# A graph layer's gathered rows: five or four tiles a batch by columns instead of four or three, more column groups on VectorE, and the weighting in three pieces

## The chip, the cores and the metric

The kernel runs on one core of a Trainium2 chip. The metric is the time of one execution on the device, in microseconds (us); a time of a kernel is the median of its runs. The profile is one execution of its own.

## The reference

The layer has 12,500 nodes with 128 features and 412,500 edges, sorted by target (`dst`). Cut to what matters:

```python
x = x + layer(relu(layernorm(x)), [src, dst], edge_attr)

def layer(node_features, edge_indices, edge_features, W_node, W_edge, a):   # 4 heads of 32
    h = (node_features @ W_node.T).reshape(num_nodes, H, HD)
    e = (edge_features @ W_edge.T).reshape(num_edges, H, HD)
    h_src, h_tgt = h[src], h[tgt]
    att = jnp.sum(jnp.concatenate([h_src, h_tgt, e], axis=-1) * a, axis=-1)
    att = jnp.where(att > 0, att, 0.2 * att)
    m = jnp.maximum(segment_max(att, tgt), 0.0)
    ex = jnp.exp(att - m[tgt])
    denom = segment_sum(ex, tgt) + (num_edges - deg)[:, None] * jnp.exp(-m)
    w = ex / denom[tgt]
    return segment_sum(w[:, :, None] * h_src, tgt)
```

So each edge needs one row of `h` (its source's), a score, the largest score of its target, and a weighted sum into its target.

## The kernel before

**Tiles and batches.** A first stage makes a table of rows (144 floats: four heads and their scores) for all nodes. Then the edges go by in 461 chunks of 896; seven chunks make a batch, 66 batches in all. A batch holds 49 tiles of 128 rows × 144, in one of three buffers `hs`. Four ways fill a tile of `hs` with the rows of its sources:

- POOL's indirect DMA, `gather_tile` (L334), one instruction a tile: 44 tiles in an odd batch, 45 in an even one.
- SP, row by row (`row_by_row`, DMAs at L864): one tile a batch, 128 rows in an odd batch and 96 in an even one, in groups of 32 rows. One group goes ahead of each load of edge features `eft` (`load`, L760), on the same queue.
- By columns: the normalised node features lie transposed in on-chip memory (`features`), so that one node is one column. `column_by_column` takes a group of 32 source numbers into registers (a load at L852) and copies 32 columns, one by one, into `turned`: by DVE (L883) or by ACT (L885). `put_back` then multiplies a tile of `turned` with the weights on PE (L904) into `more`, of which there is one, and ACT copies it into `hs` (L905). `TURNED = 4`: an odd batch has four such tiles (16 groups), an even one three and a quarter (13 groups; the quarter, 32 rows of SP's tile, goes through L909 and L911).
- The tile by rows and the tiles by columns are left out of POOL's list (`apart_of`, `clear_rows`).

**A batch on the engines.** The program has one hand-written order for all engines. In iteration `b`: SP loads indices, near rows and penalties; POOL waits at a small memset (`gate`, L819) until the scatter of batch b − 2 is done, and gathers batch b + 1; SP goes through the rows of batch b + 2 and its `eft`. Then `weigh(b)` on DVE: logits (L1000, L1001), sums (L1004, four), the leaky step (L1007, L1008), a scan up (L1009), a scan down (L1012), the subtraction (L1014). ACT takes the exponential (L1016, four), and DVE goes on with L1018 (four), a transpose that waits for the exponential (L1021) and L1026.

Behind it come the put-backs of batch b + 2 (`later`), one by one: the first behind the exponential, the second behind ACT's loads of `near_dst`, then a group of columns, the third, and the fourth where there is one. Then `collect(b − 1)`: 16 copies on ACT (L1120) that take the sums of the batch before out of PE's accumulator, with a group of columns in the middle. Then `scatter(b)`: DVE multiplies the rows with the weights (L1089) in two pieces, tiles 0 to 2 and 2 to 7 of each chunk, and 28 matmuls of PE (L1095 in the profile) sum them by target; each waits for its piece and, the first, for `collect`. DVE makes addresses (L842) and masks (L789) for later batches. Behind every even batch's scatter two batches are merged (`close`; ACT L1167 and L1168, DVE L1151 to L1194). At the end of the iteration come ACT's remaining groups, and PE begins the scores of batch b + 2 (L935, L938), which wait for its `eft`.

**Who copies the groups.** `OF_SCALAR = (10, 9)`: ACT has 10 groups in an even iteration and 9 in an odd one: one ahead of the last put-backs, one inside `collect`, two ahead of an even iteration's merge or with the rest, and the rest at the end, ahead of the next exponential. `OF_VECTOR = (5, 5)`: DVE has one group behind each of the first five places of `BEHIND`: "rows" and "first" (behind the two pieces of the product), "near" (behind L789), "hot" (behind L958) and "down" (behind the second scan L1012, ahead of the subtraction L1014).

The exponential of a batch thus stands behind all of ACT's groups of the iteration before, and DVE's subtraction behind its group.

Of the kernel before, what the change touches and what calls it, by code (L numbers as in the profile page):

```python
# [25 lines left out]
T = 7  # L26
# [41 lines left out]
FIRST = 2  # L68
# [6 lines left out]
PLACE = 88736  # L75
HOME = 11104
ALL = NBT - 7
TURNED = 4
OF_SCALAR = (10, 9)
OF_VECTOR = (5, 5)  # L80
BEHIND = ("rows", "first", "near", "hot", "down", "up")


def tiles_of(c):
# [75 lines left out]
def kernel(  # L160
# [195 lines left out]
    with (  # L356
# [140 lines left out]
        def of_vector(u):  # L497
            return (u.s.b0 + u.i0) // XS % 3 == 0 and u.m == XS
# [425 lines left out]
    def on_half(s, step):  # L924

        tc.declare_no_dep(step.ins, group=f"z{s.b + 1}", reason="the next batch has other partitions")
        tc.add_manual_dep(step.ins, s.made.ins.name, mybir.DependencyInfo(mybir.DependencyClass.Sync, mybir.DependencyReason.DATA))
# [63 lines left out]
    def weigh_part(s, t0, t1):  # L991

        zst, att, up, m, both = s.zst, s.att, s.up, s.m, s.both
        own = s.hs.rearrange("p (t q) (h k) -> p t q h k", t=T, h=H)[:, t0:t1, :s.chunks, :, AW - 1]
        e0, e1 = t0 * P, t1 * P

        def grouped(what, g):
            return what.rearrange("r (t g i) -> r g t i", g=NQT, i=R)[:, g, t0:t1, :]

        nc.vector.tensor_copy(logits[:, t0:t1, :s.chunks * H].rearrange("p t (q h) -> p t q h", h=H), own)  # L1000
        nc.vector.transpose(zst[:, t0:t1, :].rearrange("p t i -> p (t i)"),  # L1001
                            logits[:, t0:t1, :].rearrange("p t i -> p (t i)"))
        for g in range(NQT):
            on_half(s, nc.vector.tensor_tensor(grouped(up, g), grouped(s.z, g),  # L1004
                                               zst[g * R:(g + 1) * R, t0:t1, :], op=OP.add))
        z = s.z[:, e0:e1]
        nc.vector.tensor_scalar(att[:, e0:e1], up[:, e0:e1], 0.2, None, op0=OP.mult)  # L1007
        on_half(s, nc.vector.tensor_tensor(z, up[:, e0:e1], att[:, e0:e1], op=OP.max))  # L1008
        on_half(s, nc.vector.tensor_tensor_scan(up[:, e0:e1], s.pen[:, e0:e1], z, 0.0, op0=OP.add, op1=OP.max))  # L1009
        of_vector("up")  # L1010
        mp = m[:, e0:e1]
        nc.vector.tensor_tensor_scan(mp[:, ::-1], s.pen[:, e1:e0:-1], up[:, e0:e1][:, ::-1], 0.0, op0=OP.add, op1=OP.max)  # L1012
        of_vector("down")
        on_half(s, nc.vector.tensor_tensor(att[:, e0:e1], z, mp, op=OP.subtract))  # L1014
        for g in range(NQT):
            nc.scalar.activation(both[g * R:(g + 1) * R, 0, t0:t1, :], grouped(att, g), AF.Exp)  # L1016
        for g in range(NQT):
            nc.vector.scalar_tensor_tensor(both[g * R:(g + 1) * R, 1, t0:t1, :], grouped(s.pen[:, 1:], g), -1.0 / BIG,  # L1018
                                           grouped(up, g), op0=OP.mult, op1=OP.mult)
        if t1 - t0 == T:  # L1020
            nc.vector.transpose(both_ps.rearrange("p w t r -> p (w t r)"), both.rearrange("p w t r -> p (w t r)"))  # L1021
        else:
            for w in range(2):
                nc.vector.transpose(both_ps[:, w, t0:t1, :].rearrange("p t r -> p (t r)"),  # L1024
                                    both[:, w, t0:t1, :].rearrange("p t r -> p (t r)"))
        nc.vector.tensor_copy(own, both_ps[:, 1, t0:t1, :s.chunks * H].rearrange("p t (q h) -> p t q h", h=H))  # L1026
# [56 lines left out]
    def scatter(s):  # L1083

        flat = s.hs.rearrange("p i c -> p (i c)")
        blocks = flat.rearrange("p (t x k) -> p t x k", t=T, k=HS)
        for t0, t1 in ((0, FIRST), (FIRST, T)):
            rows = blocks[:, t0:t1, :, :HB]
            nc.vector.tensor_tensor(  # L1089
                rows, rows, ex_ps[:, t0:t1, :CB * H, None].to_broadcast([P, t1 - t0, CB * H, HB]), op=OP.mult)  # L1090
            of_vector("rows" if t1 == T else "first")
            for t in range(t0, t1):
                for g in range(2):
                    at = (t * CB + g * NEXT) * ROW + g * HALFROW
                    scattered[s.b] = nc.tensor.matmul(  # L1095
                        wide_ps[:, g, :], s.hot[:, t, g * NEXT:g * NEXT + SB, :].rearrange("p q r -> p (q r)"),
                        flat[:, at:at + SPAN], start=(t == 0), stop=(t == T - 1))
                    if s.fence:
                        tc.declare_no_dep(scattered[s.b].ins, s.fence, reason="DVE's products are behind that wait")
# [171 lines left out]
    def batch(b):  # L1271
        if b not in batches:
            s = batches[b] = Batch()
            s.b = b
            s.hs = None
            s.turned, s.groups = None, []
            s.c0 = chunk_of(b)
            s.chunks = chunk_of(b + 1) - s.c0
        return batches[b]
# [27 lines left out]
    with tc.manual_schedule():  # L1307
# [20 lines left out]
        for b in range(NBT - 1):  # L1328
            s = batch(b)
            batches.pop(b - 3, None)  # L1330
            soon = b >= NBT - ALONE
            if AHEAD <= b + 3 < NBT:
                batch(b + 3).ends = index(b + 3)
            load_near(batch(b + 1))
            load_pen(batch(b + 1))
            due = [k for k in (b - 1,) if k >= 0 and k < NBT - ALONE and merge_of(k)[1] == k]
            for k in due:
                for b0, n, behind in parts():
                    if behind == k and not held_x:
                        held_x[b0] = load_part(work, b0, n)  # L1340
            if b:
                gather(batch(b + 1), scattered.get(b + 1 - RING))
            if b + 2 < NBT:
                open_rows(batch(b + 2))
            if b + 4 < NBT:
                number(batch(b + 4))
            if b + 2 < NBT:
                load(batch(b + 2), True)
            if b == NBT - 2:
                choose(batch(b + 1))  # L1350
                mark(batch(b + 1))
            spare[ENG.Activation] = OF_SCALAR[b % 2] if b <= BOTH else 0
            chosen.clear()
            chosen.update(BEHIND[:OF_VECTOR[b % 2] if b <= BOTH else 0])
            weigh(s)
            later = batch(b + 2) if b + 2 < NBT else None
            if later:
                put_back(later, 0)
            if b < NBT - 2:
                mark(s)  # L1360
            for store in stores:
                store()
            stores.clear()
            if later:
                load_dst(later, nc.scalar)
                put_back(later, 1)
            of_scalar()
            if later:
                put_back(later, 2)
                put_back(later, 3)  # L1370
            if 1 <= b <= NBT - ALONE:
                collect(batch(b - 1))
            if later:
                put_back(later, TURNED)
            scatter(s)
            if b + 4 < NBT:
                address(batch(b + 4))
            if b < NBT - ALONE:
                choose(batch(b + 1))
            if 1 <= b <= NBT - ALONE:  # L1380
                if merge_of(b - 1)[1] == b - 1:
                    of_scalar(2)
                close(batch(b - 1))
            if soon:
                collect(s)
                if b == NBT - 2:
                    first_part(batch(b + 1))
            if NBT - ALONE <= b < NBT - 2:
                choose(batch(b + 1))
            if b == NBT - 3:  # L1390
                mark(batch(b + 1))
            of_scalar(spare[ENG.Activation])
            assert all(k.b > b + 3 for k, _, _ in turning), b
            if b + 2 < NBT:
                begin(batch(b + 2))
            if b == COUNTED:
                add_windows(count_windows())
            if b == 1:
                nc.scalar.copy(acc.rearrange("p q d -> p (q d)"), carry_m.to_broadcast([P, WQ * AW]))
                near_columns()  # L1400
            if soon:
                for b0, n, behind in parts():
                    if behind == b and not held_x:
                        held_x[b0] = load_part(work, b0, n)
                close(s)
            if b + 2 < NBT:
                clear_rows(batch(b + 2))
# [294 lines left out]
```

## Time and profile before

| what | us |
|---|---|
| median of 3 runs | 6768.51 |
| lowest and highest | 6765.73 and 6787.56 |
| the profiled execution | 6719.83 |
| its span (first to last instruction) | 6718.1 |

The busy times are of the span. A row of the waits names the engine, the tile and line that waited, the engine, tile and line that released it, and then the total in us, how often, and the longest. "issue" as the releaser means that the engine waited for nothing that the profile shows. A row of a timeline has the start, the duration, the engine, line and operation, the tiles written and read, and how many instructions are drawn together; in brackets the engine's idle time ahead of it and its releaser. DVE, ACT, POOL, PE and SP are the five engines; SPq and ACTq are DMA starts on their queues. Line numbers of the changed kernel are those of before up to L1008 and one higher from L1009 on.

### The profile page before, as it was taken

The page shows a single profiled execution, that of the slowest core. Times are in us where ns is not written, and L with a number is a line of the kernel's source. Part 1 is how long each engine was busy: PE and PEld are TensorE (multiplying, and loading weights), DVE is VectorE, ACT ScalarE, POOL GpSimd, SP SyncE. Part 2 cuts the span into 40 slices and gives each one's busy share as a digit, 9 for nine tenths or more (in the row PEclk, how much of TensorE's full clock was granted, in tenths as well). Part 3 has the DMA queues.
Part 4 walks back from the last instruction along what each step waited for, and adds up shares of the span by engine and source line. Part 5 has one row for each costly group of instructions (what it writes and reads, how often), then busy time and mean ns, then how long its engine had stood idle before and what let it go on. Part 6 is the DMA issues. An engine that isn't in the chain of part 4 may idle for free. (4 is left out here: it accounts for less than half of the span.)

```text
span 6718.1 us, 65140 instructions
## 1 busy us (share of the span) xinstructions
PE 1803.4 (27%) x4569; PEld 724.3 (11%) x4569; DVE 2718.8 (40%) x13514; ACT 2583.9 (38%) x20492; POOL 2797.8 (42%) x3018
## 2 busy tenths in 40 slices
PE   4223123223123232222232232133123223312323
PEld 3101001011011011010011011011011001101111
DVE  4434334344344243353343344344334334434445
ACT  4134334334344344344344344344334434433420
POOL 4453443343443443533533443443453353344351
PEclk8566566566566566665666566566566566656666
DMA  4322222222222222222222222222222222222221
GB/s 115 94 61 58 61 61 64 61 61 62 57 63 65 59 64 60 64 65 57 64 66 61 65 66 61 62 63 61 67 64 65 59 61 67 62 66 65 64 66 43
DMA packets 225620, 432.22 MB, mean 64 GB/s; under 512 B 92316, under 2 KB 125094, under 8 KB 225144
## 3 DMA queue, kind: packets, MB, share of 16 engines
q0 software_dynamic: 94240, 216.84, 13.5%
q1 hardware_dynamic: 100664, 145.09, 7.4%
q10 hardware_dynamic: 30240, 66.08, 2.8%
q14 instruction: 438, 3.59, 0.2%
q8 instruction: 38, 0.62, 0.0%
HBM read 412.21 MB, written 15.53 MB: 64 GB/s over the span
## 5 line engine op out<-in xcount | busy, mean ns | idle before, releaser
L885 ACT COPY turned<-features 128x1 f32 x18624 | 2053.1, 187 | 3473.0 <-issue 3469.9
L334 POOL DMA_INDIRECT hs<-table,ends x2887 | 2734.6, 947 | 1006.8 <-issue 895.0
L819 POOL MEMSET gate<- 128x1 f32 x63 | 6.2, 99 | 2758.7 <-PE pa L1095 2751.6
L1095 PE MATMUL pa<-hs,hot 128*128 128x504 f32 x1820 | 937.0, 680 | 531.5 <-ACT r L1120 478.6
L904 PE MATMUL more<-wall,turned 128*128 128x144 f32 x430 | 155.5, 457 | 3011.5 <-ACT hs L905 2985.0
L883 DVE COPY turned<-features 128x1 f32 x9888 | 681.8, 142 | 691.9 <-issue 689.8
L1021 DVE STREAM_TRANSPOSE exr<-both 128x448 f32<-128x448 f32 x65 | 42.9, 660 | 1530.4 <-ACT both L1016 1529.8
L1095 PEld LDWEIGHTS pa<-hs,hot 128*128 128x128 f32 x1820 | 398.5, 223 | 1045.4 <-issue 505.2
L1089 DVE TENSOR_TENSOR hs<-hs,exr 128x1848 f32<-128x1848 f32 (+1 forms) x130 | 456.6, 3515 | 0.0
L904 PEld LDWEIGHTS more<-wall,turned 128*128 128x128 f32 x430 | 91.5, 265 | 3093.8 <-ACT hs L905 3027.1
L938 PE MATMUL z<-eft,wa 128*32 128x512 f32 (+1 forms) x792 | 354.4, 592 | 61.5 <-DMA eft<-in_ef 61.4
L935 PE MATMUL z<-eft,wa 128*64 128x512 f32 (+1 forms) x132 | 85.6, 738 | 960.1 <-DMA eft<-in_ef 814.5
L1014 DVE TENSOR_TENSOR a<-z,a 32x896 f32<-32x896 f32 (+1 forms) x67 | 71.7, 1070 | 643.5 <-issue 643.3
L1120 ACT COPY r<-pa 32x70 f32<-32x70 f32 (+1 forms) x1040 | 263.6, 253 | 119.3 <-PE pa L1095 88.2
L1004 DVE TENSOR_TENSOR up<-z,zst 32x224 f32<-32x224 f32 (+2 forms) x268 | 104.3, 389 | 429.8 <-PE z L795 418.9
L795 PE MATMUL z<-near_dst,near_rows 128*32 128x512 f32 (+1 forms) x528 | 214.7, 550 | 30.5 <-DVE run L1154 22.6
L1018 DVE SCALAR_TENSOR_TENSOR both<-pen_sb,up 32x224 f32<-32x224 f32 (+2 forms) x268 | 100.3, 374 | 202.2 <-issue 201.7
L1016 ACT ACTIVATE both<-a 32x224 f32<-32x224 f32 (+2 forms) x268 | 102.8, 384 | 172.1 <-DVE a L1014 126.1
L789 DVE TENSOR_TENSOR near_dst<-near_dst,least 128x1792 f32<-128x1792 int32 x66 | 132.4, 2006 | 20.3 <-DMA near_dst<-in_dstc 20.3
L958 DVE TENSOR_TENSOR hot<-exr,key 128x1568 f32<-128x1568 f32 x65 | 116.4, 1791 | 59.3 <-PE pa L1095 57.1
L1009 DVE TENSOR_TENSOR_SCAN up<-pen_sb,z 32x896 f32<-32x896 f32 (+1 forms) x67 | 133.6, 1994 | 2.3
L1194 DVE TENSOR_TENSOR acc<-acc,up 128x70 f32 x461 | 105.1, 228 | 70.7 <-issue 48.6
(203 smaller groups left out, 1503.4 us busy)
## 6 DMA issues: line engine op xcount, KB each, us to landing
hs<-table SPq DMA_DIRECT2D x7072, 0.6 KB
eft<-in_ef SPq DMA_DIRECT2D x231, 448.0 KB
near_dst<-in_dstc ACTq DMA_DIRECT2D x128, 448.0 KB
hs<-table,ends POOLq DMA_INDIRECT x2887
near_rows<-near SPq DMA_DIRECT2D x461, 0.5 KB
pen_sb<-pens SPq DMA_DIRECT2D x66, 98.1 KB
xg<-in_xh SPq DMA_DIRECT2D x13, 448.0 KB
out<-xg SPq DMA_DIRECT2D x13, 448.0 KB
```

Source lines behind the costliest of these rows:

```text
L334: load = nc.gpsimd.indirect_dma_start(out=rows, out_offset=None, in_=of[:, :], in_offset=bass.IndirectOffsetOnAxis(ap=at, axis=0), engine_ ...
L789: nc.vector.tensor_tensor(hot, s.near_dst.bitcast(I32), least[:, s.b, :, None].to_broadcast([P, 2, CE]), op=OP.is_equal)
L795: s.made = own_half(s, nc.tensor.matmul(s.z[:, part], near_rows[:, s.b % 2, k, :], hot[:, k, part], start=False, stop=(k == 1), skip_group ...
L883: nc.vector.tensor_copy(s.turned[:, i:i + 1], column)
L885: nc.scalar.copy(s.turned[:, i:i + 1], column)
L904: nc.tensor.matmul(back_ps, s.turned[:, i * P:(i + 1) * P], wall, start=True, stop=True)
L938: s.made = own_half(s, nc.tensor.matmul(s.z[:, part], wa3[:, j + s.b % 2 * (SB + 1), :], s.eft[:, j, part], start=False, stop=(j == NEXT - ...
L958: nc.vector.tensor_tensor(s.hot.rearrange("p t q r -> p (t q) r"), rows_ps[:, None, :].to_broadcast([P, T * CB, W]), key[:, :, None].to_br ...
L1009: on_half(s, nc.vector.tensor_tensor_scan(up[:, e0:e1], s.pen[:, e0:e1], z, 0.0, op0=OP.add, op1=OP.max))
L1089: nc.vector.tensor_tensor(rows, rows, ex_ps[:, t0:t1, :CB * H, None].to_broadcast([P, t1 - t0, CB * H, HB]), op=OP.mult)
L1095: scattered[s.b] = nc.tensor.matmul(wide_ps[:, g, :], s.hot[:, t, g * NEXT:g * NEXT + SB, :].rearrange("p q r -> p (q r)"), flat[:, at:at ...
L1120: nc.scalar.copy(r[h * W:(h + 1) * W, q:q + NEXT * len(of) - NEXT + 1:NEXT, :], block)
```

## The change

An odd batch gets five tiles by columns and an even one four (and the quarter): 20 and 17 groups instead of 16 and 13. POOL gathers one tile fewer in each: 43 and 44. ACT gets 10 groups in the odd iteration too. DVE gets 9 and 8 groups instead of 5 and 5: the new places are "middle", behind a new middle piece of the product (which has now tiles 0 to 2, 2 to 4 and 4 to 7), "up", behind the first scan, "leaky", ahead of it, and, in the even iteration alone, "end", behind the merge. A put-back is added ahead of `collect`.

```diff
-TURNED = 4
-OF_SCALAR = (10, 9)
-OF_VECTOR = (5, 5)
-BEHIND = ("rows", "first", "near", "hot", "down", "up")
+TURNED = 5
+OF_SCALAR = (10, 10)
+OF_VECTOR = (9, 8)
+BEHIND = ("rows", "first", "near", "middle", "hot", "down", "up", "leaky", "end")
...
         on_half(s, nc.vector.tensor_tensor(z, up[:, e0:e1], att[:, e0:e1], op=OP.max))
+        of_vector("leaky")
         on_half(s, nc.vector.tensor_tensor_scan(up[:, e0:e1], s.pen[:, e0:e1], z, 0.0, op0=OP.add, op1=OP.max))
         of_vector("up")
...
-        for t0, t1 in ((0, FIRST), (FIRST, T)):
+        for t0, t1 in ((0, FIRST), (FIRST, 2 * FIRST), (2 * FIRST, T)):
...
-            of_vector("rows" if t1 == T else "first")
+            of_vector("rows" if t1 == T else "middle" if t0 else "first")
...
                 put_back(later, 2)
                 put_back(later, 3)
+                put_back(later, 4)
             if 1 <= b <= NBT - ALONE:
                 collect(batch(b - 1))
...
                 mark(batch(b + 1))
+            of_vector("end")
             of_scalar(spare[ENG.Activation])
```

On DVE, the weights of an even batch, from the copy of the logits to the subtraction, stood so before (`turned<-features` are the column copies, `numbers` the load of their registers):

```order
L1000 COPY logits<-hs 128x7x28
L1001 STREAM_TRANSPOSE zst<-logits 128x224
L1004 TENSOR_TENSOR up<-z,zst 32x7x32 x4
L1007 TENSOR_SCALAR a<-up 32x896
L1008 TENSOR_TENSOR z<-up,a 32x896
L1009 SCALAR_TENSOR_TENSOR up<-pen_sb,z 32x896
L1012 SCALAR_TENSOR_TENSOR a<-pen_sb,up 32x896
L852 TENSOR_LOAD numbers
L883 COPY turned<-features 128x1 x32
L1014 TENSOR_TENSOR a<-z,a 32x896
```

and now so:

```order
L1004 TENSOR_TENSOR up<-z,zst 32x7x32 x4
L1007 TENSOR_SCALAR a<-up 32x896
L1008 TENSOR_TENSOR z<-up,a 32x896
L852 TENSOR_LOAD numbers
L883 COPY turned<-features 128x1 x32
L1010 SCALAR_TENSOR_TENSOR up<-pen_sb,z 32x896
L852 TENSOR_LOAD numbers
L883 COPY turned<-features 128x1 x32
L1013 SCALAR_TENSOR_TENSOR a<-pen_sb,up 32x896
L852 TENSOR_LOAD numbers
L883 COPY turned<-features 128x1 x32
L1015 TENSOR_TENSOR a<-z,a 32x896
```

Two groups more, of 32 copies each, stand between the sums L1004 and the subtraction, one on either side of the first scan.

On ACT, from the exponential of an odd batch to the copies of the sums, the order before was

```order
L1016 ACTIVATE both<-a 32x224 x4
L905 COPY hs<-more 128x144
L780 DMA near_dst<-in_dstc 128x1x896 x2
L905 COPY hs<-more 128x144
L852 TENSOR_LOAD numbers
L885 COPY turned<-features 128x1 x32
L905 COPY hs<-more 128x144 x2
L1120 COPY r<-pa 32x35 x2
```

and is now

```order
L1017 ACTIVATE both<-a 32x224 x4
L905 COPY hs<-more 128x144
L780 DMA near_dst<-in_dstc 128x1x896 x2
L905 COPY hs<-more 128x144
L852 TENSOR_LOAD numbers
L885 COPY turned<-features 128x1 x32
L905 COPY hs<-more 128x144 x3
L1121 COPY r<-pa 32x35 x2
```

One put-back more stands ahead of the copies of the sums.

## The prediction

> **What bounds the kernel now.** I read the busy times first, then the list of waits, and then one batch on each engine's timeline. The busy times name no bound; the fullest engine works 42% of 6718.1 us:
>
> ```profile
> span 6718.1 us, 65140 instructions
> PE 1803.4 (27%) x4569; PEld 724.3 (11%) x4569; DVE 2718.8 (40%) x13514; ACT 2583.9 (38%) x20492; POOL 2797.8 (42%) x3018
> ```
>
> The waits (engine, tile and line, releaser, then total, count and longest in us) say who waits for whom:
>
> ```profile
> ACT turned L885 <- issue: 3469.9, 3284, 2.9
> POOL gate L819 <- PE pa L1095: 2751.6, 62, 61.9
> DVE exr L1021 <- ACT both L1016: 1529.8, 60, 31.9
> PE z L935 <- DMA eft<-in_ef: 814.5, 26, 68.7
> DVE a L1014 <- issue: 643.3, 60, 11.1
> PE pa L1095 <- ACT r L1120: 478.6, 61, 12.9
> ```
>
> POOL, which gathers, waits 2751.6 / 62 = 44 us a batch at its gate for the scatter of an older batch. DVE waits 25 us a batch for ACT's exponential. ACT waits for nothing but the issue of its one-column copies, 3469.9 us in all. One batch of POOL (start, duration, idle time before):
>
> ```profile
> 3099.54 0.10 POOL L819 MEMSET gate<- 128x1 f32 x1 [47.32 <-PE pa L1095]
> 3100.40 0.94 POOL L334 DMA_INDIRECT hs<-table,ends  x1 [0.76 <-issue]
> ...
> 3155.33 0.94 POOL L334 DMA_INDIRECT hs<-table,ends  x1 [0.30 <-issue]
> ```
>
> Gathers follow each other every (3155.33 − 3100.40) / 44 = 1.248 us, and the 45 last to 3156.27. ACT in the same batch:
>
> ```profile
> 3068.47 0.78 ACT L1016 ACTIVATE both<-a 32x224 f32<-32x224 f32 x2
> 3070.08 0.28 ACT L905 COPY hs<-more 128x144 f32<-128x144 f32 x1
> 3071.30 0.28 ACT L905 COPY hs<-more 128x144 f32<-128x144 f32 x1 [0.94 <-PE more L904]
> ...
> 3077.68 0.28 ACT L905 COPY hs<-more 128x144 f32<-128x144 f32 x1 [0.94 <-PE more L904]
> 3077.86 2.08 ACT L1120 COPY r<-pa 32x35 f32<-32x35 f32 x8
> ...
> 3083.66 2.13 ACT L1120 COPY r<-pa 32x70 f32<-32x70 f32 x8
> ...
> 3094.58 3.06 ACT L885 COPY turned<-features 128x1 f32 x32 [0.94 <-issue]
> 3098.59 3.06 ACT L885 COPY turned<-features 128x1 f32 x32 [0.94 <-issue]
> 3102.60 2.41 ACT L885 COPY turned<-features 128x1 f32 x25 [0.95 <-issue]
> 3105.41 0.19 ACT L885 COPY turned<-features 128x1 f32 x1 [0.40 <-issue]
> ...
> 3163.61 1.67 ACT L885 COPY turned<-features 128x1 f32 x17 [0.51 <-issue]
> ...
> 3165.66 0.78 ACT L1016 ACTIVATE both<-a 32x224 f32<-32x224 f32 x2
> ```
>
> A group of 32 copies costs 3098.59 − 3094.58 = 4.01 us. About 6 us after the gate the same copies come one in 0.7 to 1.4 us, until 3163.61 − 3156.27 = 7.3 us after the last gather has ended: I call this the slow stretch. Behind it ACT finishes its groups in 3165.66 − 3163.61 = 2.1 us, and only then the exponential is due. The next gate waits for the scatter, and the scatter for ACT:
>
> ```profile
> 3085.84 13.58 PE L1095 MATMUL pa<-hs,hot 128*128 128x504 f32 x28 [8.20 <-ACT r L1120]
> ```
>
> So a batch is a ring: gate, gathers, end of the slow stretch, rest of ACT's groups, exponential, put-backs, sums out, scatter (3085.84 − 3068.47 = 17.4 us after the exponential), next gate. The batches do not all run so:
>
> ```profile
> L1016 ACT ACTIVATE both<-a x88: 383/387/390, 611.6 to 2754.3; 32x224 f32<-32x224 f32 x88
> L1016 ACT ACTIVATE both<-a x148: 383/387/389, 2868.3 to 6436.9; 32x224 f32<-32x224 f32 x148
> 1426.91 1.97 PE L935 MATMUL z<-eft,wa 128*64 128x512 f32 x2 [65.85 <-DMA eft<-in_ef]
> 1362.81 59.45 SPq L864 DMA_DIRECT2D hs<-table  x32
> ```
>
> Four activations are one batch, and the last starts some 1.2 us behind the first. Batches 3 to 24 take (2754.3 − 1.2 − 611.6) / 21 = 102.0 us each (204.0 a pair), batches 25 to 61 take 99.1 (198.2 a pair). In the earlier ones PE waits for `eft`, which SP loads behind 32 single rows that took it 59.45 us in the slow stretch: there SP sets the pace.
>
> **The change part by part, for a pair of batches.** *One gather fewer in each batch.* POOL waits 44 us a batch, so its own time is worth nothing; but the gathers' end sets the slow stretch's. It ends 1.248 us earlier, in which ACT had done one copy that it now does later for 0.09 us: −1.2 each, −2.3 a pair.
>
> *A tenth ACT group in the odd iteration (9 become 10; the even one keeps 10).* It lies behind the slow stretch, where ACT's rest decides: 4.01 us, if it is done at full pace. Bounds: 0, where ACT is not what ends last, and 32 × 1.4 = 45 us, if it were all in the slow stretch, which the gathers' end excludes. I take +4.0.
>
> *One put-back more in each batch.* It stands ahead of the sums, so between exponential and scatter. Two follow each other 3071.30 − 3070.08 = 1.22 us apart: PE's product 0.85, ACT's copy 0.28, one PSUM tile between them. +2.4 a pair.
>
> *The product in three pieces.* Before, DVE has it done when PE is released by ACT, 3085.84:
>
> ```profile
> 3075.86 2.07 DVE L1089 TENSOR_TENSOR hs<-hs,exr 128x1848 f32<-128x1848 f32 x1
> 3079.78 4.96 DVE L1089 TENSOR_TENSOR hs<-hs,exr 128x4620 f32<-128x4620 f32 x1
> 3084.66 2.02 DVE L883 COPY turned<-features 128x1 f32 x32
> ```
>
> The pieces are 2.07, 2.07 and about 4.96 − 2.07 = 2.9 us, with a group of 2.02 us between; the last ends near 3086.7, while PE needs it only after 16 of 28 matmuls, some 7 us behind 3085.84. Zero. The group moves what follows on DVE by 2 us: near an even batch's merge ACT waits for DVE's sums, which I put at +0.4 a pair (between 0 and 2.0).
>
> *DVE's groups behind the long operations of the weights.* Today one group stands there, and it runs into the slow stretch:
>
> ```profile
> 3108.55 2.01 DVE L1012 TENSOR_TENSOR_SCAN a<-pen_sb,up 32x896 f32<-32x896 f32 x1
> 3110.75 1.43 DVE L883 COPY turned<-features 128x1 f32 x22 [0.20 <-issue]
> 3114.62 0.15 DVE L883 COPY turned<-features 128x1 f32 x1 [1.26 <-issue]
> 3134.92 1.08 DVE L1014 TENSOR_TENSOR a<-z,a 32x896 f32<-32x896 f32 x1 [10.35 <-issue]
> 3167.27 0.66 DVE L1021 STREAM_TRANSPOSE exr<-both 128x448 f32<-128x448 f32 x1 [26.37 <-ACT both L1016]
> ```
>
> The first 22 copies are quick, then 1.40 us each, and 10.35 us of issue follow before the subtraction L1014, which the exponential needs. It ends at 3136.0, some 29 us before ACT asks (3165.66). Now three groups stand ahead of L1014, 96 copies. In the odd iteration the first starts where the first scan stood, 2 us ahead of 3108.55; some 24 quick copies and 8 slow ones (11 us) end near 3119, the issue gap near 3130, the scan near 3132. The slow stretch then has 3163.61 − 1.2 − 3132 = 30 us, in which the second group gets its load and 18 to 20 of 32 copies. From there DVE has left 14 × 0.063 + 2.0 (scan) + 2.0 (group) + 1.1 (L1014), with 0.4 for loads: 6.4 us. ACT's rest is 2.1 + 4.0 = 6.1 in the odd iteration: DVE late by about 0.3. In the even one ACT had 9.1 us left:
>
> ```profile
> 3059.40 0.84 ACT L885 COPY turned<-features 128x1 f32 x8 [0.50 <-issue]
> ...
> 3068.01 0.56 ACT L885 COPY turned<-features 128x1 f32 x5
> ```
>
> There DVE has a ninth group, behind the merge, which starts the weights 2 to 3 us later and lets more of them fall into the slow stretch: some 10 more copies or one more issue gap stay for its end. Bounds: 0, if DVE ends inside ACT's 9.1 us, and +10, if the gap of 10.35 us comes once more behind the slow stretch; I take +0.9, near the lower end since gaps were seen in the slow stretch alone. Together +1.2 a pair. The cover that the groups use up is the 26.37 us; if it were smaller by 10, the cost would be the upper bound.
>
> *The sum.* −2.3 + 4.0 + 2.4 + 0.4 = +4.5 a pair without DVE. The 18 pairs of batches 25 to 61: +81. The 10.5 pairs of batches 3 to 24 come to ACT's pace of 198.2 + 4.5 = 202.7, where SP had 204.0: −14. The first batches and the end: +2, by half a pair. DVE: 1.2 × 30 = +36. In all +105 on the profiled execution's 6719.8: 6825. That execution is 48.7 us under the median of 6768.5; at 204.0 − 198.2 = 5.8 us a pair, eight or nine more pairs at SP's pace would account for it (an estimate). At 202.7 both paces have nearly met, so I expect 6825 against the median too: +0.8%.
>
> **Rivals.**
> *Faster: SP stays the pace in most batches.* If `eft` comes last everywhere, the tenth ACT group and the put-backs fall into a wait, and only the shorter slow stretch counts, which lets SP's slow rows end earlier: −1.2 a pair, if it helps in one batch of the two, or −2.4. For it: the 26 long waits at L935, and a median that is nearer to that pace. Against it: the 36 batches without such a wait. From 6768.5, 30 pairs × −1.8 = 6715, between 6697 and 6732.
>
> *No change.* By the sum without DVE's term 6720 + 69 = 6789, and from there to 6753 if half of the tenth group (2.0 × 18 = 36 us) fits where ACT waits for DVE at the merge. The Trainium skill, "Runtime: NRT & Kernel Launch", section Instruction fetch mechanics, says that instruction fetch is hidden by the issue floor: by it copies added to DVE would cost 2.0 us wherever they stand, and DVE would not be late. The trace speaks against it in this place: the same copy takes 0.063 us at 3110.75 and 1.40 us at 3114.62, released by issue alone.
>
> *Much slower: DVE's chain ends last.* If L1014 has its gap of 10.35 us once more behind the slow stretch, less ACT's rest, in the even iteration alone: +9 × 30 = 270, so 7060. It decides from the point where the second group (behind the first scan) is not issued by the slow stretch's end.
>
> *The gathers slow down.* With two groups more beside them each gather could wait for DVE's copies: if POOL stood still during each, 2 × 2.02 us a batch, 62 × 4 = +250. In the trace POOL's gathers stay 1.25 us apart beside DVE's 22 quick copies:
>
> ```profile
> 3110.38 0.95 POOL L334 DMA_INDIRECT hs<-table,ends  x1 [0.30 <-issue]
> 3111.63 0.94 POOL L334 DMA_INDIRECT hs<-table,ends  x1 [0.30 <-issue]
> ```
>
> So I give it little. The Trainium skill, "GPSIMD Engine Reference", section Specifications, names the shared SBUF interfaces and their contention with DVE in a 2-port mode; these two rows show none.
>
> **How the numbers follow.** Chances: the forecast (ACT's ring, DVE a little late) 0.57; SP's pace 0.17; no change 0.17; DVE's chain 0.06; slow gathers 0.03. About 0.3% (20 us) is what a measurement of this kernel can tell from no change: same is 6748 to 6789. The forecast's own bounds: tenth group halved and no DVE term give 6753 (of which a part counts as same), +4 a pair for DVE 6910. The range reaches down into SP's case, 6715, and up to 6920; what lies beyond is DVE's chain, the slow gathers, and the lower half of SP's case. Faster 0.19, same 0.21, slower 0.60.
>
> **What would show it.** In the profile after: the same 1.25 us between gathers; L1014's counterpart ending no longer 29 us ahead of the exponential but within a few us of it, and the wait of L1021's counterpart for ACT down from 25 us to a few, or turned into a wait of ACT for DVE; the scatter 18.6 us after the exponential in odd batches instead of 17.4; periods of about 102 and 101 us for odd and even. Wrong would be: periods under 99 us, a long wait of PE for `eft` in nearly every batch, ACT waiting over 5 us for the subtraction, or a gap other than 1.25 us between gathers.

## The result, and the profile after

The changed kernel took 6885.34 us (median of 4 runs, 6881.31 to 6888.67) against 6767.12 us of the kernel before (four runs now, 6764.60 to 6787.56): a ratio of 1.0168, with a 95% interval from 1.0147 to 1.0189. It is slower, as forecast, by 118 us. The forecast was 6825, a rise of 57 us: the range holds the measured time, but the rise is twice the one forecast. Its profiled execution took 6888.67 us. The page's first part, after:

```profile
span 6886.9 us, 73667 instructions
PE 1803.2 (26%) x4693; PEld 751.3 (11%) x4693; DVE 3266.9 (47%) x20555; ACT 2691.6 (39%) x21514; POOL 2739.2 (40%) x2956
```

DVE has 548 us of work more than before and ACT 108, POOL 59 less; none of these is the difference of the times. Some rows of the waits, after:

```profile
ACT turned L885 <- issue: 3477.6, 3233, 3.2
POOL gate L819 <- PE pa L1096: 3005.9, 62, 74.5
DVE turned L883 <- issue: 2069.1, 1896, 2.0
...
ACT both L1017 <- DVE a L1015: 178.2, 35, 86.1
...
PE z L935 <- DMA eft<-in_ef: 154.4, 3, 62.3
```

Three things are to be seen. POOL waits longer at its gate, 48.5 us a batch instead of 44.4: the gather that it was spared (1.25 us) and the longer batch both went into its wait. DVE's long wait for the exponential is all but gone (20.4 us instead of 1529.8), and in its place stand DVE's own slow copies (2069.1 us instead of 689.8) and ACT's wait for the subtraction. And PE's wait for `eft` has shrunk from 814.5 us to 154.4; the three waits that are left lie in the first 410 us and at 6775 us, so in batches 3 to 61 SP sets the pace nowhere any more. The exponentials, again four to a batch, in batches 3 to 24 and 25 to 61:

```profile
L1017 ACT ACTIVATE both<-a x88: 383/387/389, 634.4 to 2793.8; 32x224 f32<-32x224 f32 x88
L1017 ACT ACTIVATE both<-a x148: 383/387/390, 2907.7 to 6611.3; 32x224 f32<-32x224 f32 x148
```

A batch takes (2793.8 − 1.2 − 634.4) / 21 = 102.8 us in the first stretch and (6611.3 − 1.2 − 2907.7) / 36 = 102.8 in the second: one pace, 205.7 us a pair, where before there were two, 204.0 and 198.2. ACT around an odd batch's exponential and the next (27 and 28):

```profile
3102.80 0.65 ACT L885 COPY turned<-features 128x1 f32 x6 [0.51 <-issue]
3104.86 3.06 ACT L885 COPY turned<-features 128x1 f32 x32 [1.40 <-issue]
3108.86 3.06 ACT L885 COPY turned<-features 128x1 f32 x32 [0.94 <-issue]
3112.70 0.39 ACT L1017 ACTIVATE both<-a 32x224 f32<-32x224 f32 x1 [0.78 <-DVE a L1015]
...
3209.37 1.30 ACT L885 COPY turned<-features 128x1 f32 x13 [0.51 <-issue]
3211.63 3.07 ACT L885 COPY turned<-features 128x1 f32 x32 [0.96 <-issue]
3214.83 0.39 ACT L1017 ACTIVATE both<-a 32x224 f32<-32x224 f32 x1
```

and DVE in the same time:

```profile
3102.80 0.52 DVE L883 COPY turned<-features 128x1 f32 x7 [0.55 <-issue]
3103.35 2.03 DVE L1010 TENSOR_TENSOR_SCAN up<-pen_sb,z 32x896 f32<-32x896 f32 x1
3105.41 2.03 DVE L883 COPY turned<-features 128x1 f32 x32
3107.48 2.01 DVE L1013 TENSOR_TENSOR_SCAN a<-pen_sb,up 32x896 f32<-32x896 f32 x1
3109.52 2.03 DVE L883 COPY turned<-features 128x1 f32 x32
3111.58 1.09 DVE L1015 TENSOR_TENSOR a<-z,a 32x896 f32<-32x896 f32 x1
...
3213.66 1.08 DVE L1015 TENSOR_TENSOR a<-z,a 32x896 f32<-32x896 f32 x1
```

The slow stretch ends at 3102.80 and at about 3209. In the first case DVE has only come to its first scan by then; both scans, two groups and the subtraction stand behind it, 9.9 us, and ACT, done at 3111.9, waits 0.78 us for them. In the second the subtraction is done at 3214.74 and ACT's last copy at the same time: a tie. Before, the subtraction was done 29 us ahead.

PE's scatter, in batch 27 (its exponential at 3112.70):

```profile
3121.03 0.85 PE L904 MATMUL more<-wall,turned 128*128 128x144 f32 x2 [4.32 <-ACT hs L905]
3122.24 0.85 PE L904 MATMUL more<-wall,turned 128*128 128x144 f32 x2 [0.37 <-DVE hs L1090]
3131.32 15.12 PE L1096 MATMUL pa<-hs,hot 128*128 128x504 f32 x28 [8.23 <-ACT r L1121]
```

It starts 18.6 us behind the exponential instead of 17.4, still released by ACT's copies of the sums: the fifth put-back has its 1.2 us there, and the product in three pieces is not what PE waits for. (How long the 28 matmuls take differs from batch to batch, before as after: 14.3 and 14.6 us in the medians behind odd and even exponentials before, 14.6 and 14.3 after.)

### The profile page after: what moved, and what is told of

Read it like the earlier page. It is cut to its first block, busy times and chain, and to the rows that moved or that the text cites. A ratio compares the mean times of both kernels' runs of the same rounds, so it can differ in the third digit from the quotient of the medians.

```text
span 6886.9 us, 73667 instructions
## 1 busy us (share of the span) xinstructions
PE 1803.2 (26%) x4693; PEld 751.3 (11%) x4693; DVE 3266.9 (47%) x20555; ACT 2691.6 (39%) x21514; POOL 2739.2 (40%) x2956
## 5 line engine op out<-in xcount | busy, mean ns | idle before, releaser
L885 ACT COPY turned<-features 128x1 f32 x19584 | 2137.3, 187 | 3485.1 <-issue 3477.6
L334 POOL DMA_INDIRECT hs<-table,ends x2825 | 2676.0, 947 | 985.6 <-issue 869.5
L883 DVE COPY turned<-features 128x1 f32 x16864 | 1231.5, 143 | 2073.6 <-issue 2069.1
L904 PE MATMUL more<-wall,turned 128*128 128x144 f32 x554 | 214.3, 485 | 4109.3 <-ACT hs L905 4101.4
L904 PEld LDWEIGHTS more<-wall,turned 128*128 128x128 f32 x554 | 126.5, 284 | 4214.2 <-ACT hs L905 4171.2
L1004 DVE TENSOR_TENSOR up<-z,zst 32x224 f32<-32x224 f32 (+2 forms) x268 | 104.3, 389 | 479.0 <-PE z L795 306.0
L938 PE MATMUL z<-eft,wa 128*32 128x512 f32 (+1 forms) x792 | 321.3, 548 | 1.3 <-DMA eft<-in_ef 1.3
L1010 DVE TENSOR_TENSOR_SCAN up<-pen_sb,z 32x896 f32<-32x896 f32 (+1 forms) x67 | 133.6, 1994 | 186.9 <-issue 171.9
L1017 ACT ACTIVATE both<-a 32x224 f32<-32x224 f32 (+2 forms) x268 | 103.0, 384 | 224.0 <-DVE a L1015 178.2
L1000 DVE COPY logits<-hs 128x196 f32<-128x196 f32 (+1 forms) x67 | 32.9, 492 | 299.6 <-issue 289.7
L958 DVE TENSOR_TENSOR hot<-exr,key 128x1568 f32<-128x1568 f32 x65 | 116.5, 1792 | 55.5 <-PE pa L1096 53.3
L1013 DVE TENSOR_TENSOR_SCAN a<-pen_sb,up 32x896 f32<-32x896 f32 (+1 forms) x67 | 132.7, 1981 | 2.7 <-DVE turned L883 0.6
L905 ACT COPY hs<-more 128x144 f32<-128x144 f32 x277 | 76.4, 276 | 147.4 <-PE more L904 142.5
L935 PE MATMUL z<-eft,wa 128*64 128x512 f32 (+1 forms) x132 | 67.3, 593 | 178.8 <-DMA eft<-in_ef 154.4
```

The source lines that it names most:

```text
L334: load = nc.gpsimd.indirect_dma_start(out=rows, out_offset=None, in_=of[:, :], in_offset=bass.IndirectOffsetOnAxis(ap=at, axis=0), engine_ ...
L883: nc.vector.tensor_copy(s.turned[:, i:i + 1], column)
L885: nc.scalar.copy(s.turned[:, i:i + 1], column)
L904: nc.tensor.matmul(back_ps, s.turned[:, i * P:(i + 1) * P], wall, start=True, stop=True)
L938: s.made = own_half(s, nc.tensor.matmul(s.z[:, part], wa3[:, j + s.b % 2 * (SB + 1), :], s.eft[:, j, part], start=False, stop=(j == NEXT - ...
```

## The experiments

The theory (A): with slow stretches, a batch is the ring of the prediction, in which ACT's quick work, the put-backs, the slow stretch and, in the even iteration, DVE's chain up to the subtraction add up. The rival (B) differs from run to run: that only ACT counts, that gathers are free because POOL waits, that DVE's copies slow down ACT's, or that the pieces cost time.

The runs fell on four chips, and this turned out to matter more than any edit: on two of them the kernel before took 6722 and 6731 us, on the other two 4000 to 4003. I tell the runs by that. For the runs of the result no chip is on record; there the kernel before took 6767 us and has the slow stretches.

**Chips where the kernel before takes 4.0 ms.** Four variants of the changed kernel ran on the first of them. `late` moves DVE's three groups around the scans behind the four operations L1019:

```diff
-        of_vector("leaky")
...
-        of_vector("up")
...
-        of_vector("down")
...
                                            grouped(up, g), op0=OP.mult, op1=OP.mult)
+        of_vector("leaky")
+        of_vector("up")
+        of_vector("down")
```

> The changed kernel with the groups of the places leaky, up and down moved behind the four operations that follow the subtraction (so none stands ahead of the subtraction any more); the number of groups on each engine is kept. Theory A (in the iteration of even number ACT waits for DVE's subtraction, some 43 us in all, and its own groups end last elsewhere): the subtraction ends 45 us or more ahead of the exponential in every batch, ACT waits for it no more, about 1.5 us a pair less, 6842 us against 6885. Theory B (DVE's copies beside ACT's slow down ACT's issue in the slow stretch, and the wait for the subtraction is of no account): no change, 6875 to 6895, since as many copies of DVE fall into the slow stretch.

`act9` takes the tenth group of the odd iteration from ACT:

```diff
-OF_SCALAR = (10, 10)
-OF_VECTOR = (9, 8)
+OF_SCALAR = (10, 9)
+OF_VECTOR = (9, 9)
```

> The changed kernel with 9 instead of 10 groups on ACT in the odd iteration, and that group on DVE at the place end, where DVE waits for PE anyway. Theory A (ACT and DVE are nearly tied in the odd iteration: the subtraction ends 68.3 us behind the gate, the exponential starts at 69.0): only the 0.7 us up to the tie are won, 0.7 a pair, 6864 us. Theory B (ACT's groups alone set the pace there): the whole group is won, 3.5 to 4 us a pair, 6765 to 6780.

`act9near` does that too and moves DVE's three groups of the odd iteration:

```diff
         of_vector("near")
+        if s.b % 2 == 0:
+            of_vector("leaky")
+            of_vector("up")
+            of_vector("down")
```

> As act9, but in the odd iteration the groups leaky, up and down stand behind the mask of the next batch (place near), ahead of the slow stretch, where DVE waits some 11 us for PE. Theory A (tie of ACT and DVE): with DVE's chain short again the tenth group shows its full price, 3.5 to 4 us a pair, 6765 to 6780 us. Theory B (ACT's groups alone): the same as act9, since the place of DVE's groups does not matter.

`more` gives one gather a batch back to POOL:

```diff
-                        and (t, q) not in apart_of(s.b)):
+                        and (t, q) not in (apart_of(s.b)[:-1] if turned_of(s.b) else apart_of(s.b))):
...
-        if i < len(turned_of(s.b)):
+        last = len(turned_of(s.b)) - 1
+        if i < last:
             t, q = turned_of(s.b)[i]
-            nc.tensor.matmul(back_ps, s.turned[:, i * P:(i + 1) * P], wall, start=True, stop=True)
-            nc.scalar.copy(s.hs[:, t * CB + q, :], back_ps)
+            for k in (last, i) if i == 2 else (i,):
+                nc.tensor.matmul(back_ps, s.turned[:, k * P:(k + 1) * P], wall, start=True, stop=True)
+                nc.scalar.copy(s.hs[:, t * CB + q, :], back_ps)
```

> The changed kernel with one gather more a batch (45 and 44 again): the last tile by columns is gathered by POOL, while its columns are still copied and still put back, into the place of another tile ahead of that tile's own put-back, so that DVE, ACT and PE have the same work. Theory A (the end of the gathers sets the end of the slow stretch, which sets the exponential): 1.25 us a batch longer, 62 batches, some +75, 6960 us. Theory B (POOL waits 48 us a batch at its gate, so a gather costs nothing): 6885, no change.

Measured, on a chip where the kernel before took 4002.5 us: `late` 3935.0 (ratio 0.9833, 0.9814 to 0.9852), `act9` 3929.1 (0.9817, 0.9801 to 0.9833), `act9near` 3931.9 (0.9816, 0.9798 to 0.9833), `more` 4006.1 (1.0009, 0.9991 to 1.0026). None of the expectations could be tested, since the slow stretch that they speak of is missing there. So the changed kernel itself came next, with two of them.

> The changed kernel itself, unaltered, beside the variants. The runs late, act9, act9near and more came from a chip on which the kernel before took 4002 us and no slow stretch is seen, so none of their expectations could be tested there. Theory A: where the slow stretches are (before near 6.7 ms) it is 1.5 to 2% slower than before, with a pair of batches at 205.7 us; where they are missing (before near 4.0 ms) POOL is never at its gate, the gathers set the pace, and it is as fast as late and act9, 3930 us or 1.8% faster. Theory B (the change is slower by its own work everywhere): slower than before on either.

It took 3933.5 us against 3999.5 before, a ratio of 0.9847 (0.9821 to 0.9874): on this chip the change makes the kernel faster by 1.5%. Its waits, and ACT and POOL in one batch:

```profile
ACT turned L885 <- issue: 652.2, 611, 3.0
ACT both L1017 <- DVE a L1015: 530.4, 66, 81.8
...
POOL gate L819 <- PE pa L1096: 42.2, 1, 42.2
```

```profile
1822.51 3.06 ACT L885 COPY turned<-features 128x1 f32 x32 [0.95 <-issue]
1826.57 3.06 ACT L885 COPY turned<-features 128x1 f32 x32 [0.99 <-issue]
1830.57 3.06 ACT L885 COPY turned<-features 128x1 f32 x32 [0.93 <-issue]
```

```profile
1803.42 0.94 POOL L334 DMA_INDIRECT hs<-table,ends  x1 [0.30 <-DMA near_dst<-in_dstc]
1804.35 0.12 POOL L819 MEMSET gate<- 128x1 f32 x1
...
1822.77 0.95 POOL L334 DMA_INDIRECT hs<-table,ends  x1 [0.31 <-issue]
```

The same instructions, the same gathers beside them, but a group is issued in 4.0 us throughout, and POOL passes its gate without a wait (one of 42.2 us in the whole run, instead of 62 of 48). POOL is the bound here: it goes from one batch's gathers to the next, and the gather that the change takes from it is time won.

> The same kernel as late, for a chip with slow stretches. Theory A (in the iteration of even number ACT waits for DVE's subtraction, some 43 us in all): the waits of ACT for the subtraction go, about 1.5 us a pair less than the changed kernel, 204.2 instead of 205.7. Theory B (DVE's copies beside ACT's slow down ACT's issue, the wait is of no account): 205.7 again.

> The same kernel as more (one gather more a batch, all other work kept), for a chip with slow stretches. Theory A (the gathers' end sets the slow stretch's end, and that the exponential): 2.4 us a pair more than the changed kernel, 208.1. Theory B (POOL waits 48 us a batch, so a gather costs nothing): 205.7.

`late_b` 3937.1 (0.9834, 0.9812 to 0.9856) is as fast as the changed kernel, and `more_b` 4002.4 (1.0003, 0.9986 to 1.0021) as slow as the kernel before: (4002.4 − 3933.5) / 62 batches = 1.1 us for a gather, nearly the 1.25 us in which one follows another. That ACT waits 530.4 us for the subtraction costs nothing there, as `late` shows, in which that wait is 293.2 us.

`mixed`, which has both edits, each in one half of a pair (the diffs of `act9near`, and of `late` for odd batches), was meant for a chip with slow stretches and fell on the fourth chip, without them.

> Two edits to the changed kernel that meet in different halves of a pair. From an odd to an even exponential: ACT has 9 groups instead of 10, and DVE's three groups around the scans stand behind the mask instead, ahead of the gathers. From an even to an odd one: DVE's three groups stand behind the four operations that follow the subtraction. Theory A, where there are slow stretches (before near 6.7 ms): the first half falls from 102.1 by the price of the tenth group, 3.5 to 4.0 us, and the second from 103.5 by ACT's wait for the subtraction, about 1.5 us, so a pair of 200.2. Theory B (DVE's copies beside ACT's hold up ACT's issue, wherever they stand): the first half falls by under 2 us, the second not at all. Where there are no slow stretches (before near 4.0 ms): the same as the changed kernel, 3930 us.

It took 3929.9 us (0.9825, 0.9805 to 0.9845), as said for that case.

**Chips with slow stretches.** `twice` repeats a put-back of the changed kernel:

```diff
                 put_back(later, 2)
+                put_back(later, 2)
```

> The changed kernel with the third put-back of each batch done twice (the second writes the same values). Theory A (each put-back ahead of the copies of the sums lies between exponential and scatter): 1.2 us a batch, 62 batches, +75, 6960 us, and the scatter starts 19.8 and 18.6 us behind the exponential. Theory B (DVE's product in three pieces or PE ends last there): no change, 6885.

6940.1 us, where the kernel before took 6722.1 (ratio 1.0315, 1.0286 to 1.0345). Its exponentials in batches 25 to 61, its scatter in batch 27 and its wait for the subtraction:

```profile
L1017 ACT ACTIVATE both<-a x148: 383/387/390, 2928.2 to 6668.4; 32x224 f32<-32x224 f32 x148
```

```profile
3154.30 14.12 PE L1096 MATMUL pa<-hs,hot 128*128 128x504 f32 x28 [8.22 <-ACT r L1121]
```

```profile
ACT both L1017 <- DVE a L1015: 210.6, 34, 86.6
```

The scatter starts 3154.30 − 3134.47 = 19.8 us behind the exponential, 1.2 later, and a pair takes 2 × (6668.4 − 1.2 − 2928.2) / 36 = 207.7 us, 2.0 more than 205.7 where A said 2.4. (The changed kernel itself was not run on this chip; against its median of the result it is 55 us where A said 75.) B, by which nothing would change, is out. ACT's wait for the subtraction has grown (210.6 instead of 178.2): in the iterations that lead to an odd batch's exponential ACT's own groups end 68.1 us behind the gate instead of 70.7 (medians of batches 27 to 61), the subtraction 71.1 instead of 71.6. ACT came earlier to it, DVE hardly did.

`pieces` is the kernel before with the product in three pieces and nothing else:

```diff
-        for t0, t1 in ((0, FIRST), (FIRST, T)):
+        for t0, t1 in ((0, FIRST), (FIRST, 2 * FIRST), (2 * FIRST, T)):
```

> The kernel before with the product in three pieces and nothing else (no group behind the middle piece). Theory A (DVE has the product done ahead of PE's need): no change against the kernel before, 6767, within 20 us. Theory B (the pieces make PE's scatter start later or run with gaps): over 1 us a batch, 6830 or more.

6727.9 against 6722.1, a ratio of 1.0007 (0.9993 to 1.0020): no difference. B is out here too.

`best` was built on A: put-backs between the copies of the slow stretch, the fifth behind the copies of the sums, more groups on DVE, none ahead of the subtraction. PE's scores of batch b + 2 also begin ahead of ACT's last groups. Of its edit, the constants and one line:

```diff
-OF_SCALAR = (10, 10)
-OF_VECTOR = (9, 8)
-BEHIND = ("rows", "first", "near", "middle", "hot", "down", "up", "leaky", "end")
+OF_SCALAR = (10, 8)
+BEHIND = ("rows", "first", "near", "middle", "hot", "late")
+BEHIND_MASK = (1, 5)
+BEHIND_WEIGHTS = (1, 4)
+AHEAD_BACK = (((2, 24), (3, 8), (3, 16), (3, 24)), ((4, 24), (5, 8), (5, 16), (5, 24)))
...
-            of_scalar(spare[ENG.Activation])
+            of_scalar(spare[ENG.Activation], between)
```

> A version from what was found so far: of the five put-backs four go between ACT's column copies of the iteration before, eight copies apart, where the slow stretch lies, and the fifth behind the copies of the sums; ACT has 8 groups in the odd iteration; DVE has no group ahead of the subtraction, one behind the weights of even batches and four behind those of odd ones, and five behind the mask in odd iterations. Theory A (ACT's quick work and the slow stretch make up the period, DVE has room ahead of the slow stretch in odd iterations and behind the subtraction): the exponential to scatter falls from 18.6 and 17.4 to some 14 us, a pair from 205.7 to about 189, 6385 us where the kernel before takes 6720 to 6770. Theory B (SP's rows with eft or DVE take over as the bound): a pair at 198 to 204, no better than before. Without slow stretches POOL's gathers stay the bound: the same as the changed kernel, 3930 us.

It fell on a chip of the first kind: 3951.5 us (0.9876, 0.9855 to 0.9897), faster than before, slower than the changed kernel. A second run fell on one with slow stretches.

> The same kernel as best, for a chip with slow stretches. Theory A (ACT's quick work and the slow stretch make up the period): the scatter starts some 14 us behind the exponential instead of 18.6 and 17.4; from an odd to an even exponential ACT, with two groups fewer, is done by the end of the slow stretch, 91 to 93 us instead of 102.1; from an even to an odd one 97 to 99 instead of 103.5; a pair at 189 to 191 and 6385 to 6450 us, 4 to 5% under the kernel before. Theory B (SP's rows with eft, or DVE's groups, take over): PE waits for eft in most pairs, or ACT for the subtraction, and a pair stays at 198 to 204, 6700 or more. Where there are no slow stretches (before near 4.0 ms): 3950 us again, 1.2% under before.

6986.3 us, where the kernel before took 6730.6: a ratio of 1.0378 (1.0354 to 1.0402), the slowest of all. The scatter did come earlier, 14.6 and 15.4 us behind the exponential, but a pair takes longer, from batch 26 on 2 × (6710.9 − 1.2 − 3068.4) / 35 = 208.1 us:

```profile
L1021 ACT ACTIVATE both<-a x144: 383/387/390, 3068.4 to 6710.9; 32x224 f32<-32x224 f32 x144
```

DVE behind the mask in an odd iteration (the fourth group runs into the slow stretch after 18 copies), and at the end of the slow stretch one such iteration earlier:

```profile
3194.73 2.01 DVE L888 COPY turned<-features 128x1 f32 x32
3198.23 2.03 DVE L888 COPY turned<-features 128x1 f32 x32 [1.49 <-issue]
3201.75 2.03 DVE L888 COPY turned<-features 128x1 f32 x32 [1.49 <-issue]
3205.27 1.18 DVE L888 COPY turned<-features 128x1 f32 x18 [1.49 <-issue]
```

```profile
3055.66 2.03 DVE L888 COPY turned<-features 128x1 f32 x32 [1.49 <-issue]
...
3058.09 0.50 DVE L1007 COPY logits<-hs 128x196 f32<-128x196 f32 x1 [0.24 <-DVEq L316]
...
3067.21 1.08 DVE L1019 TENSOR_TENSOR a<-z,a 32x896 f32<-32x896 f32 x1
```

and ACT there:

```profile
3068.39 0.39 ACT L1021 ACTIVATE both<-a 32x224 f32<-32x224 f32 x1 [8.69 <-DVE a L1019]
...
3154.68 0.28 ACT L912 COPY hs<-more 128x144 f32<-128x144 f32 x1 [10.31 <-issue]
```

Two prices were wrong. Groups that follow each other on DVE take 3.5 us each, not 2.0: 1.49 us of issue stand between two of them, and none where a long operation stood between (the rows of DVE in batch 27 above). I take this for the load of their registers, which no run tried. So the five groups did not fit ahead of the slow stretch, the weights waited behind the fourth and fifth until it was over, and ACT waited 8.7 us for the subtraction. And a put-back inside the slow stretch had 10.31 us of issue ahead of it, some seven slots of 1.4 us, where I had reckoned one. The two halves of a pair suffer differently: from an odd to an even exponential the median is 102.8 us, 8.7 of them this wait, so that DVE ends last as theory B has it; from an even to an odd one it is 105.3 (103.5 in the changed kernel) without any wait for the subtraction, and ACT's own groups, the put-backs among them, end 75.7 us behind the gate instead of 70.7. What fewer groups on ACT are worth by themselves the run does not show. No version was found that beats both kernels on both kinds of chip.

## Why the prediction was right, point by point

The direction, the ring and most sizes held. The step that failed is the cover of DVE's term in one half of a pair; together with the start it is why the rise is larger than forecast.

*The put-back, +1.2 a batch.* Shown: the scatter starts 18.6 and 17.4 us behind the exponential instead of 17.4 and 16.2, and `twice` adds 1.2 us there again and 2.0 a pair.

*The pieces, zero.* Shown by `pieces`.

*The odd half of a pair (from an odd to an even exponential): −1.2 + 4.0 + 1.2 + 0.3 = +4.3.* The median of 17 such halves in batches 26 to 60 went from 97.6 to 102.1 us: +4.5. Inside it, from the gate to the exponential, 65.8 became 69.0, +3.2 against −1.2 + 4.0 + 0.3. The trace has the two terms near these sizes: the last gather ends 55.5 us behind the gate instead of 56.7, and from 7.3 us behind it ACT needs 6.1 us to the exponential instead of 1.7 (medians of 18). DVE's 0.3 did not arise: the subtraction ends 0.7 us ahead of the exponential. The sum fits; that a gather and ACT's tenth group have just these prices where there are slow stretches was not tried by itself, since the runs for it fell on the other chips.

*The even half (from an even to an odd exponential): −1.2 + 1.2 + 0.4 + 0.9 = +1.3.* The median of 18 went from 100.4 to 103.5 us: +3.1. This is the step that failed. The prediction let DVE end 9.1 + 0.9 = 10.0 us behind the slow stretch, and so it does: from the gate the subtraction ends at 71.6 us (median), 61.5 of which are up to 7.3 us behind the last gather. The 0.9 was picked between 0 and 10, so that it met this end is in part luck, and the way there is another than the prediction had. Not some 10 copies more are left behind the slow stretch, but both scans, two groups and the subtraction, since DVE's ninth group runs into the slow stretch and the gap in the issue comes ahead of the logits (30 such waits, 289.7 us):

```profile
3253.38 1.55 DVE L883 COPY turned<-features 128x1 f32 x24 [1.99 <-issue]
...
3274.00 0.49 DVE L1000 COPY logits<-hs 128x196 f32<-128x196 f32 x1 [10.10 <-issue]
```

What was mis-sized is the cover. It was read from a single batch, whose ACT had 9.1 us left behind the slow stretch. The median of its kind is 69.75 − 62.8 = 6.9, and that batch was the longest of the 18. With 6.9 the term would have been 3.1 instead of 0.9 and the half +3.5. In `twice`, on another chip, the term is seen at this size: ACT's own groups end 68.1 − 61.5 = 6.6 us behind that point and the subtraction 9.6, and ACT waits 3.0 us for it in the median. In the changed kernel's run ACT's own groups came later as well (69 copies behind the slow stretch in the median instead of 60; why, the record does not show), so that its visible wait for the subtraction is only 1.1 us in the median, and 43 us in the 28 such halves of batches 4 to 60 without that of batch 24, 1.5 us each. By the trace the half would be shorter by that much without DVE's groups ahead of the subtraction; the run for it, `mixed`, fell on a chip without slow stretches, so this is argued and not shown.

*The start.* I gave the first batches +2 us; batch 3 came 634.4 − 611.6 = 22.8 us later. In the first batch nothing covers the weights, and ACT waits 86.1 us for the subtraction instead of 75.1. DVE there, before and after:

```profile
305.65 0.33 DVE L842 TENSOR_SCALAR numbers<-numbers,factor 4x128 int32<-4x128 int32 x1 [0.22 <-DMA numbers<-in_sources]
305.91 0.48 DVE L1000 COPY logits<-hs 128x196 f32<-128x196 f32 x1
...
318.09 1.08 DVE L1014 TENSOR_TENSOR a<-z,a 32x896 f32<-32x896 f32 x1
```

```profile
314.29 0.33 DVE L842 TENSOR_SCALAR numbers<-numbers,factor 5x128 int32<-5x128 int32 x1 [1.17 <-DMA numbers<-in_sources]
314.55 0.48 DVE L1000 COPY logits<-hs 128x196 f32<-128x196 f32 x1
...
331.42 1.08 DVE L1015 TENSOR_TENSOR a<-z,a 32x896 f32<-32x896 f32 x1
```

From the logits to the end of the subtraction it is 319.17 − 305.91 = 13.3 us before and 332.50 − 314.55 = 18.0 after: the two groups more around the scans cost 4.7 us at once. The other 8.6 us by which the subtraction is later are there before the logits begin, behind the load of `numbers`; why that landed later no run shows. From batch 0 to batch 3 another 9.5 us are added, 3.2 a batch.

*The sum.* On the profiled execution: 18 pairs at +7.5 (+135 instead of +103 with DVE's share), the 10.5 pairs of batches 3 to 24 at 205.7 instead of 204.0 (+18 instead of −1), the start +23 (instead of +2), the end some −6: +170, and measured 6888.7 − 6719.8 = 169. Against the median it is 118, since the median of the kernel before lies 47 us above its profiled execution. The prediction put this gap down to more pairs at SP's pace; no run tests that, and on the two other chips with slow stretches the kernel's medians, 6722 and 6731 us, lie near the profiled execution.

*The rivals.* SP's pace: refuted, the waits for `eft` are gone from batches 3 to 61. Slow gathers: refuted, behind batch 26's scatter the first gather starts at 3042.21, the last of 43 at 3094.64, 1.248 us apart beside 51 copies on DVE where the prediction's batch had 32:

```profile
3041.35 0.10 POOL L819 MEMSET gate<- 128x1 f32 x1 [45.94 <-PE pa L1096]
3042.21 0.94 POOL L334 DMA_INDIRECT hs<-table,ends  x1 [0.76 <-DVE acc L1195]
...
3094.64 0.94 POOL L334 DMA_INDIRECT hs<-table,ends  x1 [0.30 <-issue]
```

DVE's chain much later: the issue gap of 10.35 us did not come back behind the slow stretch (L1015 follows its group at once, 3111.58). No change: copies on DVE did not cost 2.0 us wherever they stand; 1896 of them waited for issue. The rule of the Trainium skill ("Runtime: NRT & Kernel Launch", section Instruction fetch mechanics), that fetch is hidden by the issue floor, fits the two chips on which a group takes 4.0 us beside the gathers. It would not fit the others, with their 1.4 us a copy, if the slow issue there is a matter of fetch, which no run shows.

## What to carry to other kernels

Read the cover of a step from the median of its kind, not from the batch whose rows lie before you: here the one batch was off by 2.2 us of 6.9, which is the size of that half's miss (1.8 us). When a late chain is handed more work, add up what is left behind the end of the stretch that hides it, and compare it with what the other engine has left; two engines that tie there make each one's saving worth little. And before a bound is believed, look at the kernel on a second chip: the same program was bound by a ring through ACT's slow issue on one and by POOL's gathers on another, and the change had opposite signs.

## What the runs showed of the hardware that was not expected

The slow stretch goes with the chip, or with what else differs between the runs on these four chips, and not with the program: on two chips copies beside gathers are issued every 0.7 to 1.4 us and the kernel before takes 6722 and 6731 us; on two others they are issued every 0.09 us and it takes 4000 us, with the same 1.25 us between gathers. The records do not show why, and no run tried it. Two things on record do not explain it: the changed kernel has the same number of packets on the instruction queues on both kinds of chip (503 and 39), and though TensorE's mean granted clock is 0.61 to 0.63 on the one kind and 0.70 on the other, a group of 32 copies on ACT outside the slow stretch is busy for 3.06 us on both. In a slow stretch single operations can stand behind a long gap: up to 11.2 us of issue ahead of the first scan L1010 in the changed kernel (171.9 us in 29 waits), and 10.31 ahead of a put-back's copy in `best`. The traces have no instruction of the engine in these gaps; that instructions which the profile leaves out take a slot each there is a guess.
